# Splitting the first feed-forward's down projection twice for all blocks, with its weights combined in the attention phase and the second feed-forward's on VectorE

## The chip, the core and the metric

One core of a Trainium2 chip runs the kernel. The metric is device time in microseconds (us), the median of several executions. TensorE (PE in the profile) multiplies, VectorE (DVE) and ScalarE (ACT) work element by element, GpSimd (POOL) does too, and SyncE (SP) issues most of the DMAs, in the order in which they stand in its queue.

## The reference

Eight sequences of 512 tokens with 512 channels in float32 go through four residual layers: cross attention with a linear kernel, a feed-forward, a second cross attention, and a feed-forward of merged experts.

```python
def ffn0(x, proj1, b1, proj2, b2):                 # 512 -> 2048 -> 512
    return gelu(x @ proj1.T + b1) @ proj2.T + b2

def ffn1(x, ...):                                  # 8 groups, 192 hidden units each
    w_tg = ...                                     # a token's share for each group, from a router
    gu, dn = gate_up_proj[dominant_experts], down_proj[dominant_experts]
    gate, up = split(einsum("th,goh->tgo", x, gu))
    return einsum("tg,tgi,ghi->th", w_tg, silu(gate) * up, dn)

x = x + tanh(g_xattn[0]) * linear_attention(layernorm(x), ctx)
x = x + tanh(g_ffn[0])   * ffn0(layernorm(x), ...)
x = x + tanh(g_xattn[1]) * cross_attention(layernorm(x), ctx, mask)
x = x + tanh(g_ffn[1])   * ffn1(layernorm(x), ...)
```

## The kernel before

The work is cut into 24 blocks: the attention layer for each of the eight sequences (`xa0`), then the first feed-forward for each (`ff0`), then the second cross attention with the second feed-forward (`ff1`). While one block multiplies, the next one is prepared: its tokens are normalised on VectorE (`normed`, L426), with the reciprocal standard deviation `rstd` from GpSimd (L442), transposed on TensorE (`turn`), and combined into `S` (`token_combinations`).

All large matrix products use Strassen's scheme in its Winograd form: a product of 2 x 2 quarters takes seven smaller products, numbered 1 to 7, in place of eight. It needs sums and differences of the quarters on both sides. On the weight side they are made once and stored in DRAM; on the token side they are made for each block. `combining` (L233) is the weights' four subtractions.

An `ff0` block has four up units (`Ff0Up`), each with seven products of 128 x 256 results (L789), and one down unit. Their hidden activations are the quadrants a11, a12, a21, a22 of `inner`; `combine_inner` (L825) adds s1 and s2 and turns a21 into the difference. The products of a unit run in the order 1, 2, 6, 5, 7, 4, 3, with the last two of a unit put behind the first of the next unit.

There are two forms of the down unit. `Down` (L890) multiplies seven times with 16 matmuls of 128 x 256 results, over 8 chunks (L905). `SplitDown` (L928) applies the scheme a second time to each of the seven products: 49 small products with 4 chunks each, 28 matmuls of 128 x 128 results for each of the seven (L984). For that, `combine` makes four subtractions of the activations for each product (L969 to L972), `at_once` adds the small results together (L998, L1003, L1007), and the weights are read as one continuous stream, 49 tiles of 256 KB a block. The seven products run in the order `SPLIT_ORDER["ff0"]` = 1, 4, 2, 6, 5, 7, 3. Product 2 reads a12, product 6 reads s2. The first two `ff0` blocks (`ONCE = 2`) use `Down`, the other six `SplitDown`; all `ff1` blocks use `SplitDown` with 3 chunks.

Each product's weights come from DRAM into a ring of 16 tiles (`ring`, L132) on SyncE's queue, 16 tiles ahead of TensorE. When a product is issued, the load for the tile that it frees follows.

The combined weights are made by builders, generators that are stepped now and then:

- In the attention phase `tick` steps `build_weights("ff0", ...)` at every third product. It loads raw weights into ring tiles, GpSimd combines them (four operations of 128 x 512), and SyncE stores the seven results: four up units, then four down chunks for the once-split form.
- In the `ff0` phase `build_stream("ff0", ...)` loads the down weights again, in a tile of seven parts (`build_tile`), combines them on GpSimd, combines the result once more (four operations of 128 x 896, L412 to L419), and stores seven slices of 448 KB in the stream. After that the same is done for the second feed-forward: six up units, then three down chunks. It is stepped at every second or third up product.

GpSimd also adds the output bias to each block's tokens (L581), and makes `rstd`. SyncE's queue carries, besides weights and builds, the attention's denominators: `over<-z` writes 1/denominator to DRAM and `spread<-over` reads it back to all partitions (L1132, L1140). A tile scheduler orders the instructions of the engines; an engine named in `in_order` keeps the order of the program, and SyncE always does here. The functions touched, as they are before the change:

Of the kernel before, what the change touches and what calls it, by code (L numbers as in the profile page):

```python
# [21 lines left out]
F32 = mybir.dt.float32  # L22
# [8 lines left out]
P = 128  # L31
# [37 lines left out]
def flamingo_kernel(  # L69
# [60 lines left out]
    RING = 16  # L130

    def ring(name):  # L132
        return work.tile([P, 2, H2], F32, tag="ring", name=name, bufs=RING)

# [125 lines left out]
    raw_g = []  # L260
    for c in range(NC):
        raw_g.append(ring(f"raw_g{c}").rearrange("p n f -> p (n f)"))
        nc.sync.dma_start(out=raw_g[c], in_=wg[ts(c, P), :])
# [6 lines left out]
    def order_gate():  # L270
# [12 lines left out]
    SPLIT_ORDER = {"ff0": (1, 4, 2, 6, 5, 7, 3), "ff1": (2, 4, 1, 6, 5, 7, 3)}  # L283
# [3 lines left out]
    ONCE = 2  # L287
# [7 lines left out]
        (ph, kind, i, q): dram.tile([P, 2, H2], F32, tag=f"{ph}_{kind}{i}_{q}", name=f"{ph}_{kind}{i}_{q}")  # L295
        for ph, kind, n in (("ff0", "up", 4), ("ff0", "down", 4), ("ff1", "up", 6))
# [58 lines left out]
    def build_weights(ph, tile7):  # L355

        todo = {
            "ff0": (("up", raw_p1, 4), ("down", raw_p2, 4)),
            "ff1": (("up", raw_gu, 6),),
        }[ph]  # L360
        todo = [(kind, raw, i) for kind, raw, n in todo for i in range(n)]

        def load(kind, raw, i):
            t = tile7(f"{ph}_{kind}{i}")
            raw(t, i)
            return t

        if ph == "ff1":
            for kind, raw, i in todo:
                t = load(kind, raw, i)  # L370
                yield
                yield from in_twos(combining(nc.gpsimd, t))
                for q in range(7):
                    nc.sync.dma_start(out=store[ph, kind, i, q], in_=t[q])
                yield
            return
        t = load(*todo[0])
        yield
        for n, (kind, raw, i) in enumerate(todo):
            following = load(*todo[n + 1]) if n + 1 < len(todo) else None  # L380
            yield from combining(nc.gpsimd, t)
            for q in range(7):
                nc.sync.dma_start(out=store[ph, kind, i, q], in_=t[q])
            yield
            t = following

    def in_twos(steps):
        for n, _ in enumerate(steps):
            if n % 2:
                yield  # L390

    def build_stream(ph, raw, tile7):

        place = [SPLIT_ORDER[ph].index(m) for m in (1, 5, 2, 3, 6, 7, 4)]
        for i in range(SPLIT_CHUNKS[ph]):
            t = tile7(f"{ph}_down{i}")
            w = [t[:, k] for k in place]
            raw(w, i)
            yield
            yield from in_twos(combining(nc.gpsimd, w))  # L400

            b = t.rearrange("p k n (h q) -> p k n h q", q=P)
            b11, b12, b21, b22 = (b[:, :, n, h] for n in range(2) for h in range(2))

            def keep(m, w):
                nc.sync.dma_start(out=stream[ph][:, :, SPLIT_INNER.index(m), i, :], in_=w)

            sub = ALU.subtract
            for m, w in ((1, b11), (2, b21), (3, b22)):
                keep(m, w)  # L410
            yield
            nc.gpsimd.tensor_tensor(b12, b12, b11, sub)  # L412
            keep(5, b12)
            yield
            nc.gpsimd.tensor_tensor(b22, b22, b12, sub)
            keep(6, b22)
            yield
            nc.gpsimd.tensor_tensor(b21, b21, b22, sub)
# [7 lines left out]
    def normed(ph, b, tag):  # L426
# [4 lines left out]
        if ph == "xa0":  # L431
            in_order.add("vector")
# [1112 lines left out]
```

## Time and profile before

| | |
|---|---|
| median of 3 runs | 2104.07 us (2101.84 to 2106.63) |
| profiled execution | 2106.83 us, span of its instructions 2104.7 us |
| TensorE busy (PE) | 2061.6 us |
| VectorE busy (DVE) | 1451.9 us |
| ScalarE busy (ACT) | 596.6 us |
| GpSimd busy (POOL) | 318.0 us |
| DMA | 485.12 MB, mean 230 GB/s |

The span is the time from the first to the last instruction. The attention phase takes up to about 418 us of it, the eight `ff0` blocks up to about 1188 us, the `ff1` blocks the rest. Matmuls are pipelined, so the durations of single ones overlap; the time of a product is the distance between starts, as the chain of waits has it. In a row of a group the parts are: line, engine and operation, output and inputs, shape, count, then busy us and mean ns of one, then the engine's idle time before it and what ended that. In a row of waits they are: who waited for whom, us in total, times, the longest.

### The profile page before, as it was taken

How to read it: one execution, taken by the hardware profiler on the slowest of the kernel's cores; microseconds unless marked ns; L12 is line 12 of the kernel's file. 1: busy time of each engine (PE TensorE's matmuls, PEld its weight loads, DVE VectorE, ACT ScalarE, POOL GpSimd, SP SyncE). 2: the span in 40 equal slices, each digit the busy share in tenths (PEclk: the TensorE clock that was granted, in tenths of full speed). 3: DMA queues.
4: the chain of work that ended last, by engine and by line, in shares of the span. 5: the costliest groups of instructions: out<-in, count | busy, mean ns of one | idle time of the engine just before them, and what ended most of it. 6: DMA issues, size and time to landing. Idle time of an engine off the chain costs nothing.

```text
span 2104.7 us, 34195 instructions
## 1 busy us (share of the span) xinstructions
PE 2061.6 (98%) x12460; PEld 1816.1 (86%) x12460; DVE 1451.9 (69%) x2727; ACT 596.6 (28%) x1236; POOL 318.0 (15%) x260
## 2 busy tenths in 40 slices
PE   8999999999999999999999999999999999999998
PEld 4778887788889998889898989898989889898988
DVE  3688777652528494868667777777777677876768
ACT  3433333222222324132334232213222222222121
POOL 3122111342413112240301010000000010100000
PEclk9999999999999999999999999999999999999999
DMA  7345633696869898888875858686776858585865
GB/s 227 120 155 155 209 132 93 214 306 220 294 220 330 285 307 288 283 298 281 297 248 190 304 163 276 198 264 214 229 237 189 283 170 293 157 284 161 269 204 169
DMA packets 306501, 485.12 MB, mean 230 GB/s; under 512 B 37024, under 2 KB 107840, under 8 KB 302240
## 3 DMA queue, kind: packets, MB, share of 16 engines
q1 hardware_dynamic: 298896, 456.18, 67.7%
q10 hardware_dynamic: 5856, 23.20, 2.9%
q0 software_dynamic: 1584, 3.57, 0.7%
q8 instruction: 100, 1.64, 0.3%
q14 instruction: 65, 0.53, 0.1%
HBM read 406.22 MB, written 76.61 MB: 229 GB/s over the span
## 4 chain that ended last, share of the span: by engine, by line
PE 74%; issue 10%; DVE 7%; DMA 4%; POOL 3%; SPq 1%; ACT 1%; ACTq 0%; POOLq 0%; DVEq 0%
PE x_ff L789 23%; PE w_ff L789 11%; PE x_ff_down L984 9%; PE w_ff_down L984 7%; PE z_ff L789 6%; PE z_ff_down L984 3%; PE v_ff_down L984 3%; PE x_ff_down L905 2%; SPq L60 1%; PE w_ff_down L905 1%; PE pt_ff L458 1%; PE pt_xa L458 1%; PE pst L609 1%; PE pr L654 1%; PE z_ff_down L905 1%
## 5 line engine op out<-in xcount | busy, mean ns | idle before, releaser
L789 PE MATMUL x_ff<-S_ff,w_ff_up 128*128 128x256 f32 x1280 | 304.5, 381 | 1.7 <-ACT u_ff L801 1.7
L789 PE MATMUL w_ff<-S_ff,w_ff_up 128*128 128x256 f32 x1280 | 303.6, 380 | 1.5 <-DVE a_ff L844 1.5
L789 PE MATMUL x_ff<-xnT_ff,w_ff_up 128*128 128x256 f32 x1280 | 294.1, 380 | 0.9 <-ACT u_ff L801 0.9
L801 ACT COPY u_ff<-x_ff 128x512 f32<-128x512 f32 x240 | 139.5, 582 | 539.2 <-PE x_ff L789 520.3
L789 PEld LDWEIGHTS x_ff<-S_ff,w_ff_up 128*128 128x128 f32 x1280 | 239.9, 190 | 42.6 <-issue 6.5
L789 PEld LDWEIGHTS w_ff<-S_ff,w_ff_up 128*128 128x128 f32 x1280 | 239.0, 190 | 34.2 <-DVE a_ff L844 2.3
L789 PEld LDWEIGHTS x_ff<-xnT_ff,w_ff_up 128*128 128x128 f32 x1280 | 238.4, 190 | 32.9 <-ACT u_ff L801 1.8
L789 PE MATMUL z_ff<-xnT_ff,w_ff_up 128*128 128x256 f32 x640 | 151.6, 379 | 0.0
L984 PE MATMUL x_ff_down<-w_ff_down,split_ff_down 128*128 128x128 f32 x1152 | 136.4, 275 | 2.8 <-DVE split_ff_down L972 1.9
L984 PEld LDWEIGHTS x_ff_down<-w_ff_down,split_ff_down 128*128 128x128 f32 x1152 | 132.2, 192 | 3.6 <-DVE split_ff_down L972 2.2
L789 PEld LDWEIGHTS z_ff<-xnT_ff,w_ff_up 128*128 128x128 f32 x640 | 119.8, 190 | 15.3
L849 ACT ACTIVATE a_ff<-a_ff,b_sb 128x256 f32<-128x256 f32 x128 | 58.1, 501 | 155.1 <-DVE a_ff L844 155.0
L984 PE MATMUL w_ff_down<-w_ff_down,split_ff_down 128*128 128x128 f32 x768 | 90.8, 275 | 1.1 <-DVE split_ff_down L972 1.1
L828 DVE TENSOR_TENSOR s_ff<-a_ff,a_ff 128x512 f32<-128x512 f32 x56 | 45.8, 819 | 65.4 <-ACT a_ff L849 65.4
L984 PEld LDWEIGHTS w_ff_down<-w_ff_down,split_ff_down 128*128 128x128 f32 x768 | 88.2, 192 | 1.3 <-DVE split_ff_down L972 1.3
L998 DVE TENSOR_TENSOR part_ff_down<-part_ff_down 128x128 f32<-128x128 f32 x245 | 72.6, 313 | 23.4 <-ACT part_ff_down L1011 17.5
L844 DVE TENSOR_TENSOR a_ff<-w_ff,u_ff 128x512 f32<-128x512 f32 x64 | 43.8, 684 | 60.1 <-ACT u_ff L801 60.1
L872 DVE SCALAR_TENSOR_TENSOR g_ff<-th_ff,x_ff 128x512 f32<-128x512 f32 x48 | 32.9, 685 | 70.4 <-ACT th_ff L871 70.4
L882 DVE TENSOR_TENSOR up_ff<-w_ff,u_ff 128x512 f32<-128x512 f32 x96 | 65.6, 683 | 17.7 <-ACT u_ff L801 17.7
L581 POOL TENSOR_TENSOR x_ff<-x_ff,b_sb 128x512 f32<-128x512 f32 x28 | 39.3, 1408 | 253.5 <-DVE xn_ff L451 253.5
L451 DVE TENSOR_SCALAR xn_ff<-x_ff,mv_ff,rstd_ff 128x512 f32<-128x512 f32 x64 | 41.2, 661 | 48.2 <-PE pt_ff L458 36.4
L984 PE MATMUL w_ff_down<-w_ff_down,s_ff 128*128 128x128 f32 x576 | 70.2, 275 | 0.0
(274 smaller groups left out, 3665.2 us busy)
## 6 DMA issues: line engine op xcount, KB each, us to landing
w_ff_down<-stream_ff SPq DMA_DIRECT2D x582, 256.0 KB
w_ff_up<-ff_up SPq DMA_DIRECT2D x560, 256.0 KB
stream_ff<-build_ff_down SPq DMA_DIRECT2D x49, 448.0 KB
x_ff<-x_ff SPq DMA_DIRECT2D x16, 1024.0 KB
share<-shares SPq DMA_DIRECT2D x64, 256.0 KB
w_ff_down<-ff_down SPq DMA_DIRECT2D x56, 256.0 KB
ff_up<-build_ff_up SPq DMA_DIRECT2D x42, 256.0 KB
spread<-over SPq DMA_DIRECT2D x32, 256.0 KB
```

Of the source, the lines that this page charges most:

```text
L451: nc.vector.tensor_scalar(xn[t], xb[:, t, :], mv[:, t, 0:1], rstd[:, t : t + 1], ALU.subtract, ALU.mult)
L458: nc.tensor.transpose(pt[:, c, :], xn[t][:, ts(c, P)], ident)
L581: nc.gpsimd.tensor_tensor(xb[:, t, :], xb[:, t, :], b2_sb, ALU.add)
L789: nc.tensor.matmul(p[:, n, :], lhsT=w[:, c, ts(n, P)], rhs=moving, **self.mark(m, 2 * n + c),)
L801: nc.scalar.copy(self.s[m], p)
L828: nc.vector.tensor_tensor(s1, a21, a22, ALU.add)
L844: nc.vector.tensor_tensor(h, p, s, ALU.add)
L849: nc.scalar.activation(h[:, n, :], p[:, n, :], AF.Gelu, bias=b1_sb[:, f : f + 1])
L882: nc.vector.tensor_tensor(u, p, s, ALU.add)
L905: nc.tensor.matmul(p[:, t, :], lhsT=a[:, k, ts(t, P)], rhs=w[k // 2][:, k % 2, :], **self.mark(m, 2 * k + t),)
L984: nc.tensor.matmul(p[bank][:, place, :], lhsT=operand[k][:, c, :], rhs=w[at // 4][:, ts(at % 4, P)], start=bank not in opened, stop=True, ...
L998: return lambda: nc.vector.tensor_tensor(m(k), m(k), m(by), ALU.add)
```

## The change

All eight `ff0` blocks use `SplitDown`, and its third and fourth products change places (6 now runs ahead of 2). `combine_inner` follows part (2, 1), product 4, instead of part (1, 2), product 3. The stream of the first feed-forward is built in the attention phase (`build_first`), alternating with the up units, stepped at two of five products; nothing of the first feed-forward is built in its own phase. The weights of the second feed-forward are built in the `ff0` phase at every up product (`build_second`), by VectorE instead of GpSimd, and those instructions keep the order of the program (`in_place`). After its loads a build waits 11 steps (`LAND`) before it combines. The bias addition goes from GpSimd to VectorE, behind each transpose. For `ff0` blocks after the second, statistics and normalisation keep the order of the program. The ring has 9 tiles in the attention phase and 7 more (`ringb`) after it; one tile `build` serves the raw gate weights, the builds, and the `ff1` sums.

```diff
-    RING = 16
+    RING, MORE = 9, 7
+    asked = {"ring": 0}
     def ring(name):
+        n = asked["ring"] % (RING + MORE) if "ringb" in bank else 0
+        asked["ring"] += 1
+        if n >= RING:
+            return bank["ringb"].tile([P, 2, H2], F32, tag="ringb", name=name, bufs=MORE)
         return work.tile([P, 2, H2], F32, tag="ring", name=name, bufs=RING)
+    def build_tile(name):
+        return work.tile([P, 7, 2, H2], F32, tag="build", name=f"build_{name}", bufs=1)
...
-    SPLIT_ORDER = {"ff0": (1, 4, 2, 6, 5, 7, 3), "ff1": (2, 4, 1, 6, 5, 7, 3)}
+    SPLIT_ORDER = {"ff0": (1, 4, 6, 2, 5, 7, 3), "ff1": (2, 4, 1, 6, 5, 7, 3)}
-    ONCE = 2
...
+    def combining_again(ph, i, t, eng):
+        b = t.rearrange("p k n (h q) -> p k n h q", q=P)
+        b11, b12, b21, b22 = (b[:, :, n, h] for n in range(2) for h in range(2))
+        def keep(m, w):
+            nc.sync.dma_start(out=stream[ph][:, :, SPLIT_INNER.index(m), i, :], in_=w)
+        sub = ALU.subtract
+        for m, w in ((1, b11), (2, b21), (3, b22)):
+            keep(m, w)
+        eng.tensor_tensor(b12, b12, b11, sub)
+        yield
+        keep(5, b12)
+        eng.tensor_tensor(b22, b22, b12, sub)
+        yield
+        keep(6, b22)
+        eng.tensor_tensor(b21, b21, b22, sub)
+        yield
+        keep(4, b21)
+        eng.tensor_tensor(b11, b22, b11, sub)
+        yield
+        keep(7, b11)
...
+    def build_first():
+        def load_up(i):
+            t = [ring(f"raw_up{i}_{q}") for q in range(7)]
+            raw_p1(t, i)
             return t
+        up = load_up(0)
+        yield
+        for i in range(4):
+            for n, _ in enumerate(combining(nc.gpsimd, up)):
+                if n == 2:
+                    t = build_tile(f"ff0_down{i}")
+                    raw_p2(placed("ff0", t), i)
                 yield
+            store_up("ff0", i, up)
+            for _ in range(2):
                 yield
+            for n, _ in enumerate(combining(nc.gpsimd, placed("ff0", t))):
+                if n % 2:
+                    yield
+            if i < 3:
+                up = load_up(i + 1)
+            yield from combining_again("ff0", i, t, nc.gpsimd)
             yield
+        streamed.add("ff0")
+    def in_place(steps):
+        while True:
+            in_order.add("vector")
+            more = next(steps, steps)
+            in_order.discard("vector")
+            if more is steps:
+                return
+            yield
+    LAND, GAP = 11, 6
+    def build_second():
+        for i in range(6):
+            t = build_tile(f"ff1_up{i}")
+            seven = [t[:, q] for q in range(7)]
+            raw_gu(seven, i)
+            for _ in range(LAND):
                 yield
+            yield from in_place(combining(nc.vector, seven))
+            store_up("ff1", i, seven)
+            for _ in range(GAP):
+                yield
+        for i in range(SPLIT_CHUNKS["ff1"]):
+            t = build_tile(f"ff1_down{i}")
+            raw_dn(placed("ff1", t), i)
+            for _ in range(LAND):
+                yield
+            yield from in_place(combining(nc.vector, placed("ff1", t)))
+            yield from in_place(combining_again("ff1", i, t, nc.vector))
+            for _ in range(GAP + 2):
+                yield
+        streamed.add("ff1")
...
+        ordered = ph == "ff0" and b > 1
-        if ph == "xa0":
+        if ph == "xa0" or ordered:
             in_order.add("vector")
...
+        def biased(t):
+            nc.vector.tensor_tensor(xb[:, t, :], xb[:, t, :], b2_sb, ALU.add)
-        for t in range(NT):
-            nc.gpsimd.tensor_tensor(xb[:, t, :], xb[:, t, :], b2_sb, ALU.add)
...
-            if (r, c) == (1, 2):
+            if (r, c) == (2, 1):
                 combine_inner(ts(self.i, 2))
...
-                self.sums = second.tile([P, 4, 7, P], F32, tag="sums", name=f"sums_{self.tag}")
+                self.sums = build_tile(f"sums_{self.tag}").rearrange(...)
...
-        if next(ticks) % 3 == 2:
+        if next(ticks) % 5 in (1, 3):
             next(builder, None)
...
-            return [Ff0Up(ph, b, i) for i in range(4)] + [Down(ph, b, NF // 2) if b < ONCE else SplitDown(ph, b)]
+            return [Ff0Up(ph, b, i) for i in range(4)] + [SplitDown(ph, b)]
...
+    bank["ringb"] = stack(tc.tile_pool(name="ringb", bufs=1, reuse_waits="tile"))
+    for _ in range(MORE):
+        next(loads)
...
-        return 5 if ph == "ff0" else 24
+        return 7 if ph == "ff0" else 24
...
         if u.kind == "up":
-            ticks += 1
-            if "ff0" not in streamed:
-                if ticks % 2 == 0:
-                    next(again, None)
-            elif ticks % 3 == 0:
-                next(builder, None)
+            next(builder, None)
```

## The prediction

> **What bounds the kernel now.** I read the page first, for the busy shares and the granted clock.
>
> ```profile
> PE 2061.6 (98%) x12460; PEld 1816.1 (86%) x12460; DVE 1451.9 (69%) x2727; ACT 596.6 (28%) x1236; POOL 318.0 (15%) x260
> ...
> PEclk9999999999999999999999999999999999999999
> ```
>
> TensorE is the bound: a saving must be a shorter matmul stream or fewer gaps in it. So I cut the span at the ends of the feed-forward blocks. The table of stretches gives length, then busy time of PE, PEld, DVE, ACT and POOL, then clock, DMA share and GB/s.
>
> ```profile
> 60.00:418.00 358.00, 344.79 (x1866) 281.69 (x1865) 270.04 (x419) 123.50 (x232) 70.06 (x59) 1.00 0.48 152
> 418.00:505.00 87.00, 85.83 (x398) 75.26 (x397) 33.16 (x43) 16.74 (x38) 28.66 (x17) 1.00 0.80 260
> 505.00:600.00 95.00, 94.22 (x445) 82.66 (x444) 41.29 (x47) 21.57 (x46) 35.58 (x21) 1.00 0.78 253
> 600.00:696.00 96.00, 94.33 (x633) 87.97 (x633) 65.42 (x121) 28.54 (x60) 25.77 (x17) 1.00 0.90 301
> 696.00:790.00 94.00, 94.00 (x634) 88.02 (x633) 65.13 (x128) 29.31 (x62) 17.81 (x13) 1.00 0.89 299
> 790.00:890.00 100.00, 96.20 (x635) 89.82 (x635) 68.37 (x128) 29.43 (x63) 21.18 (x14) 0.98 0.86 284
> 890.00:988.00 98.00, 94.81 (x631) 87.59 (x631) 73.92 (x128) 28.86 (x62) 28.18 (x16) 1.00 0.89 293
> 988.00:1083.00 95.00, 94.36 (x637) 88.04 (x636) 65.42 (x132) 29.34 (x62) 18.82 (x11) 1.00 0.88 291
> 1083.00:1188.00 105.00, 103.03 (x716) 92.56 (x714) 71.63 (x175) 43.19 (x89) 6.47 (x9) 1.00 0.70 231
> 1188.00:2105.00 917.00, 909.81 (x5687) 813.09 (x5685) 675.26 (x1347) 226.39 (x480) 45.34 (x56) 1.00 0.70 223
> ```
>
> Length less PE busy is TensorE's idle time: 13.2 us in the attention phase (first row), 13.2 us over the eight blocks of the first feed-forward (1.2, 0.8, 1.7, 0.0, 3.8, 3.2, 0.6, 2.0), 7.2 us over the whole second one. Only the first two of these stages are touched. The block at 696 has no idle at all, with VectorE at 65 of 94 us: the split form can run without gaps.
>
> Then the chain of waits where the worst block loses time (start, length, what):
>
> ```profile
> 838.04 1.73 POOL build_ff_down L236
> ...
> 840.93 1.49 DVE xn_ff L451
> 842.41 1.67 DVE split_ff_down L969
> ...
> 845.50 1.67 DVE split_ff_down L970
> ...
> 848.77 2.56 DVE split_ff_down L972
> ...
> 854.39 0.61 DVE a_ff L844
> ...
> 855.04 7.99 PE z_ff_down L984 x56
> ```
>
> While GpSimd combines weights, VectorE's own subtractions take 1.67 to 2.56 us; the page's groups and their forms have 0.68 us for the same 128x512 work without it. VectorE falls behind, a_ff (the last quadrant of hidden activations) is late, and TensorE waits before the product with it, which comes third in the down projection. After the stop that product takes 7.99 us instead of 6.25, under a granted clock of 0.79 and 0.64 in the next two stretches of 3 us: 1.7 us more. So GpSimd's 15% are not free; they are paid through VectorE.
>
> **The change, part by part.** Sums are against the profiled execution, 2106.8 us (span 2104.7 and 2.1 around it). It stands 2.8 us above the median of the runs, 2104.07; differences are carried over to the median unscaled.
>
> *1. Two down projections split twice.* From the chain:
>
> ```profile
> 471.14 6.91 PE w_ff_down L905 x32
> ...
> 763.28 6.25 PE x_ff_down L984 x56
> ```
>
> A product of the once-split form (L905) is 32 passes in 6.91 us, of the twice-split form (L984) 56 passes in 6.25 us. Seven of each: 48.4 and 43.75 us. Two blocks save 2 x 4.63 = 9.3 us of matmul stream, on the path. A rule speaks against it: the Trainium skill, "TensorE: Matmul & The Clock Gate", section "Back-to-back issue gap", has a matmul of 128 columns in a stream of weight loads at 81 ns where its columns alone would take 56, a factor of 1.46. An estimate from that: half of a 256-column pass (216 ns, 6.91/32) is 108, times 1.46 is 157 ns, times 392 passes is 61.7 us a block, 13 us more than now, 27 us slower for two. The trace has 6.25/56 = 112 ns, in this very code and with these tiles. I take the trace: -9.3.
>
> These blocks gain VectorE's work (four split combinations of 0.68 us for each of seven products, and their joining: from 33 to 41 us busy to about 65) and weight tiles, 49 of 256 KB instead of 28. The block at 696 carries both, and no idle: 0.
>
> *2. GpSimd leaves the first feed-forward.* It loses 24 bias additions there (1.41 us each in the page's group), the second combining of four down chunks, and all combining for the second feed-forward. Going to VectorE: 24 bias additions in these blocks, 24 + 12 subtractions of 128x512 at 0.68 us, and 12 of 128x896, which the trace shows on GpSimd only; between VectorE's rows of 512 (0.68) and 2048 elements (2.28) the line gives 1.08. Together 16 + 24.5 + 13 = 54 us over eight blocks, about 7 each, less the lengthening by GpSimd that ends. VectorE stays near 65 to 72 of 94 us. The second feed-forward runs at 675 of 917 with hardly more idle per block. Bounds of this step: all idle and the clock loss go (-14.9), or VectorE's added work keeps it all (0) or, with its order now fixed at these instructions, adds up to 5.
>
> *3. Order inside the down projection.* The product that needs the late quadrant moves from third to fourth place, and the combination of the other three quadrants is made one product (1.73 us) earlier. That gives the late quadrant 6.25 us more. The largest single wait, 2.5 us on a_ff L844, is this one. Normalisation kept in order no longer lets statistics for a later block stand on VectorE waiting for their load (8.3 us before the stall at 454).
>
> For 2 and 3 together: I leave the last block its 2.0 us and the others 0.3 each, 4 in all, of 13.2 + 1.7. That is -10.9; I take -10. The cover is VectorE's spare 20 us per block; without it each late combination costs its own 0.7 to 1.1 us.
>
> *4. The waits this adds.* VectorE combines in program order, so a weight that has not landed would hold everything behind it: the split combinations, then TensorE. In the trace the loads take from 605.7 to 612.7 and, for the chunk with 16 of them, from 827.1 to 838.0 until GpSimd can start. The change leaves 11 product steps of 1.73 us, 19 us. On SyncE's queue the stores of the combined weights now wait for VectorE, with the ring's weight loads behind them; the ring runs 16 tiles ahead, 14 us in the down projection (16 x 43.75/49), against a lag of 2 to 5 us. 0. The ring starts with 9 tiles and gets 7 more after one matmul product and five loads of the build: about 6 us after the first product, needed after nine (15.6 us). 0. Its tiles are as many as before after that.
>
> *5. The attention phase.* GpSimd's work here: 16 + 16 subtractions as before (1.33 us), plus 16 of 128x896. Those rows have 2.22 to 2.37 us: +37 us. The eight bias additions of the first two blocks go to VectorE (5.5 us), and four normalisations and one subtraction there get back about 4: 0. DMA: one set of loads less, 28 stores of 448 KB for 28 of 256, +1 MB over a stage whose DMA share is 0.48: 0. What the 37 us can cost shows in the waits of TensorE between 60 and 418:
>
> ```profile
> PE pt_xa L458 <- DVE xn_xa L451: 5.9, 6, 2.2
> PE x_xa_down L905 <- DVE x_xa L921: 2.9, 4, 1.0
> ```
>
> The normalised block xn_xa comes right after rstd from GpSimd, and GpSimd's combinations, held back behind rstd in its queue, all run just then: xn_xa takes 1.49 us at most against 0.54 alone. GpSimd is busy 52 us from 60 to 360 (70 to 418) with 5.9 us of such waits; 37 us more, in proportion, is +4.2. In the changed instruction order the work directly after each rstd is longer in one block, alike in most, and shorter in the last, since a chunk's second half waits for its own stores. From nothing (-1, were the timing luckier) to +10 (every 896-wide operation holding one critical VectorE operation by 0.6 us). I take +3.
>
> SyncE's queue in this phase: each chunk's 7 stores and 4 loads stand before and behind the denominators (over<-z), and in two blocks a store waiting for GpSimd stands ahead of spread<-over. I estimate a delay of 2 to 3 us; spread is issued 9 to 11 us before VectorE reads it, and about half of that is landing. 0.
>
> *6. The second feed-forward.* Sums now lie in the build's tile, one buffer as before. 0.
>
> Sum: -9.3 - 10 + 3 = -16.3. Profiled execution 2090.5; median 2087.8, so 2088.
>
> **Rivals.**
> *A. The stalls stay.* VectorE's 54 us and the added order take the place of GpSimd's disturbance; 4 stops for another 4. Then -9.3 + 3: 2097.8. For it: idle appears where VectorE has 68 to 74 busy, and the change moves towards that. Against: the gaps stand beside lengthened operations (the chain above), and the second feed-forward is as loaded without them.
>
> *B. The attention phase pays with its chain: slower.* GpSimd works in order, and rstd stands behind combinations that wait for stores, which stand on SyncE's queue behind over<-z. In the trace rstd starts every 41 us (193.6, 234.0, 277.7) and over<-z goes out 10 us after it. For the tightest chunk: stores out at +15, landed near +22, three more operations to +29, next rstd at +41: 12 us of room. Each us beyond it delays xn, the transposes and TensorE one for one. To turn 16.3 gained into over 4.2 lost takes 20.5 us more, 5 in each of four chunks: the chain must be 17 us longer than I count, in all. Then 2108.5 or more.
>
> *C. Better.* Attention costs nothing, all idle of the first feed-forward goes: -9.3 - 13.2 - 1.7 gives 2080.
>
> That the change does not do what it says is excluded by its instruction order: 392 matmuls of 128x128 replace 224 of 128x256, and only rstd is left to GpSimd in the first feed-forward.
>
> **How the numbers follow.** Main case 0.60 (2081 to 2095); A 0.20 (2094 to 2102); B or another new wait 0.12 (2101 to 2115); C 0.08 (2077 to 2081). 0.2% is 4.2 us, about what a measurement of this kernel can tell from no change, so "same" is 2099.9 to 2108.3. Faster: main, C and about 0.14 of A: 0.82. Same: the rest of A and a little of B: 0.08. Slower: 0.10. The range from 2079 to 2101 leaves out most of B and part of C.
>
> **What would show it.** Right: products of 6.25 us in the first two blocks, no GpSimd line but rstd between 418 and 1188, blocks 94 to 95 us apart, split combinations at 0.68 us, no wait for a_ff ahead of the down projection's fourth product, TensorE's idle in the first feed-forward near 4. Attention: its end within 3 us of before, xn_xa still near 1.0 us mean. Wrong: VectorE waiting on build loads, TensorE waiting on VectorE's splits as often as before (A), or rstd or xn_xa waits above 10 us in the attention phase (B).

## The result and the profile after

The changed kernel takes 2096.51 us (median of six runs, 2095.86 to 2096.93); the kernel before 2108.57 (2101.84 to 2111.61), of which three runs are those of the table before (median 2104.07) and the other three took 2110.5 to 2111.6. The ratio is 0.9947, with a 95% interval of 0.9929 to 0.9965: faster by 0.5%, some 12 us between these medians, and by the interval 7 to 15. The profiled execution of the changed kernel took 2096.49 us (span 2094.7), against 2106.8 (span 2104.7) before: 10.0 us between the spans, which is what the two traces have to account for.

First the page's busy shares and clock.

```profile
PE 2053.7 (98%) x12796; PEld 1821.1 (87%) x12796; DVE 1511.3 (72%) x2965; ACT 610.8 (29%) x1264; POOL 171.1 (8%) x164
PEclk9999999999999999999999999999999999999999
```

TensorE still bounds. VectorE has gained 59 us of work, GpSimd has lost 147. Then the table of stretches (columns: length, busy time of PE, PEld, DVE, ACT, POOL, clock, DMA share, GB/s): first the attention phase before, then the changed kernel, cut at the ends of its stages and blocks.

```profile
56.30:402.20 345.90, 332.69 (x1810) 271.02 (x1809) 266.06 (x409) 116.99 (x219) 64.53 (x51) 1.00 0.46 147
```

```profile
56.10:410.90 354.80, 336.27 (x1810) 273.89 (x1809) 281.40 (x417) 117.98 (x220) 93.40 (x65) 0.99 0.51 156
411.00:503.00 92.00, 92.00 (x617) 86.21 (x616) 55.85 (x120) 28.29 (x58) 0.00 (x0) 1.00 0.90 297
503.00:597.00 94.00, 94.00 (x635) 88.02 (x634) 66.83 (x140) 29.32 (x62) 1.03 (x1) 1.00 0.82 269
...
879.00:979.00 100.00, 96.11 (x628) 89.00 (x627) 68.82 (x141) 28.90 (x62) 1.01 (x1) 0.97 0.84 266
979.00:1074.00 95.00, 95.00 (x643) 88.99 (x643) 73.32 (x157) 29.76 (x64) 2.50 (x2) 1.00 0.89 300
1074.00:1178.00 104.00, 102.49 (x712) 91.94 (x711) 73.46 (x178) 42.75 (x90) 6.48 (x9) 1.00 0.74 244
1178.00:2095.00 917.00, 909.65 (x5686) 812.89 (x5684) 675.33 (x1347) 226.45 (x480) 45.39 (x56) 1.00 0.70 223
```

Three things are to be seen. Most blocks of the first feed-forward have no idle at all (length equals PE busy). The one from 879 lost 3.9 us and some clock. And the attention phase, first row of each table, has 18.5 us of idle where it had 13.2: it ends at 411 and no longer at 402 (the 418 given for the kernel before lies already in its first feed-forward block). The same 1810 matmuls also keep TensorE busy for 336.3 us instead of 332.7. That is the clock: both kernels have one short stretch of half clock near 81 us, the changed one two more, each right behind three us in which TensorE was busy for 1.7 and 1.1 us only.

```profile
203.00:207.00 4.00, 4.00 (x16) 3.38 (x15) 4.00 (x6) 2.80 (x6) 2.04 (x2) 0.66 0.00 0
391.00:395.00 4.00, 4.00 (x18) 3.39 (x17) 4.00 (x8) 1.16 (x3) 0.00 (x0) 0.69 0.72 265
```

Stage by stage, from the start of each stage's first `z` product to that of the next (`z_q` for attention, `z_ff` for the feed-forwards; us of the profiled executions):

| stage | before | after | difference |
|---|---|---|---|
| start | 56.3 | 56.1 | -0.2 |
| attention phase | 345.9 | 354.8 | +8.9 |
| first feed-forward | 785.6 | 766.8 | -18.8 |
| second feed-forward, to the end | 916.9 | 917.0 | +0.1 |

So the gain is that of the first feed-forward, and half of it is given back in the attention phase: 5.3 us of the 8.9 as idle, most of the rest as lost clock. TensorE's waits between 60 and 412 in the changed kernel (in total, times, longest), and what the tile's view has of the operation waited for (min/median/max in ns), first before, then after:

```profile
PE pt_xa L500 <- DVE xn_xa L491: 11.8, 8, 2.4
PE x_xa_down L956 <- DVE x_xa L972: 4.0, 3, 1.7
```

```profile
L451 DVE TENSOR_SCALAR xn_xa<-x_xa,mv_xa,rstd_xa x28: 441/996/1492, 76.2 to 326.2; 128x512 f32<-128x512 f32 x28
```

```profile
L491 DVE TENSOR_SCALAR xn_xa<-x_xa,mv_xa,rstd_xa x28: 442/1479/2296, 75.9 to 335.1; 128x512 f32<-128x512 f32 x28
```

The same VectorE instruction on the same tiles has a longest of 2.30 us instead of 1.49, and the waits on it doubled from 5.9 to 11.8. The timeline of one place shows how (start, length, operation, in brackets the idle before it):

```profile
117.01 1.01 POOL L60 TENSOR_TENSOR rstd_xa<-var_xa,neg_half 128x4 f32<-128x4 f32 x1 [34.23 <-DVE var_xa L478]
...
117.99 8.56 POOL L60 TENSOR_TENSOR build_ff_down<-build_ff_down 128x896 f32<-128x896 f32 x4
118.06 4.51 DVE L491 TENSOR_SCALAR xn_xa<-x_xa,mv_xa,rstd_xa 128x512 f32<-128x512 f32 x2
...
122.62 0.66 PE L500 MATMUL pt_xa<-ident,xn_xa 128*128 128x128 f32 x4 [1.56 <-DVE xn_xa L491]
```

GpSimd has four 128x896 subtractions queued behind rstd, 8.56/4 = 2.14 us each, and two xn_xa beside them take 4.51/2 = 2.26 us each instead of the 0.54 that they take without company (run 1): one GpSimd instruction per VectorE instruction, in step. The transposes (L500), and the products behind them, wait.

The loss in the block from 879, in the chain of waits, then VectorE's row from the timeline and the stretches after the stop:

```profile
882.19 8.97 DMA stream_ff<-build_ff_down
...
891.18 0.04 DVE build_ff_down L60
...
892.19 0.70 DVE a_ff L895
...
892.93 3.78 PE w_ff L840 x8
896.71 2.76 PE z_ff L840 x8
```

```profile
891.18 1.09 DVE L60 TENSOR_TENSOR build_ff_down<-build_ff_down 128x896 f32<-128x896 f32 x1 [7.66 <-DMA stream_ff<-build_ff_down]
```

```profile
893.00:896.00 3.00, 3.00 (x7) 2.45 (x8) 3.00 (x5) 1.54 (x4) 0.00 (x0) 0.50 0.85 230
896.00:899.00 3.00, 3.00 (x9) 2.36 (x8) 3.00 (x8) 0.00 (x0) 0.00 (x0) 0.56 1.10 355
```

VectorE's second subtraction of a second-feed-forward chunk (b22, in place) overwrites what the store issued just before is still reading, and its order is fixed: it stands until that store has landed, 7.7 us, with a_ff behind it and TensorE behind a_ff. Two products of 1.73 us then take 3.78 and 2.76: the granted clock was 0.50 and 0.56 in the two stretches of 3 us after the stop.

### The profile page after: what moved, and what is told of

The parts are those of the page before. It is cut to its first block, busy times and chain, and to the rows that moved or that the text cites. A ratio compares the mean times of both kernels' runs of the same rounds, so it can differ in the third digit from the quotient of the medians.

```text
span 2094.7 us, 35097 instructions
## 1 busy us (share of the span) xinstructions
PE 2053.7 (98%) x12796; PEld 1821.1 (87%) x12796; DVE 1511.3 (72%) x2965; ACT 610.8 (29%) x1264; POOL 171.1 (8%) x164
## 4 chain that ended last, share of the span: by engine, by line
PE 90%; DVE 4%; DMA 3%; issue 1%; POOL 1%; ACT 0%; SPq 0%; ACTq 0%; DVEq 0%; POOLq 0%
PE x_ff L840 26%; PE w_ff L840 13%; PE x_ff_down L1035 13%; PE w_ff_down L1035 8%; PE z_ff L840 6%; PE z_ff_down L1035 4%; PE v_ff_down L1035 4%; PE x_xa_down L956 2%; PE x_q L840 2%; PE pt_ff L500 1%; PE x_g L840 1%; PE pt_xa L500 1%; PE w_xa_down L956 1%; PE w_g L840 1%; DMA stream_ff<-build_ff_down 1%
## 5 line engine op out<-in xcount | busy, mean ns | idle before, releaser
L840 PE MATMUL w_ff<-S_ff,w_ff 128*128 128x256 f32 x1280 | 305.4, 381 | 4.2 <-DVE a_ff L895 4.2
L840 PE MATMUL x_ff<-S_ff,w_ff 128*128 128x256 f32 x1280 | 304.3, 380 | 0.0
L840 PE MATMUL x_ff<-xnT_ff,w_ff 128*128 128x256 f32 x1280 | 294.6, 379 | 0.0
L840 PEld LDWEIGHTS x_ff<-S_ff,w_ff 128*128 128x128 f32 x1280 | 240.5, 190 | 40.1 <-issue 5.0
L840 PEld LDWEIGHTS w_ff<-S_ff,w_ff 128*128 128x128 f32 x1280 | 240.0, 191 | 37.4 <-DVE a_ff L895 5.0
L840 PEld LDWEIGHTS x_ff<-xnT_ff,w_ff 128*128 128x128 f32 x1280 | 237.7, 190 | 31.1 <-ACT u_ff L852 0.5
L840 PE MATMUL z_ff<-xnT_ff,w_ff 128*128 128x256 f32 x640 | 152.6, 381 | 0.0
L840 PEld LDWEIGHTS z_ff<-xnT_ff,w_ff 128*128 128x128 f32 x640 | 120.7, 192 | 15.8
L1035 PE MATMUL x_ff_down<-w_ff_down,a_ff 128*128 128x128 f32 x672 | 80.4, 275 | 0.0
L1035 PEld LDWEIGHTS w_ff_down<-w_ff_down,s_ff 128*128 128x128 f32 x672 | 79.4, 192 | 0.8
```

The costliest lines, as they stand in the source:

```text
L840: nc.tensor.matmul(p[:, n, :], lhsT=w[:, c, ts(n, P)], rhs=moving, **self.mark(m, 2 * n + c),)
L1035: nc.tensor.matmul(p[bank][:, place, :], lhsT=operand[k][:, c, :], rhs=w[at // 4][:, ts(at % 4, P)], start=bank not in opened, stop=True, ...
```

## The experiments

In every case the profiled execution's stages are given beside the median, since the attention phase alone varies: in the five kernels below that leave it as the change made it (runs 4, 5, 6, 8, 9) it took 355.2 to 359.1 us in the profile, with three to five times 3.4 us of half clock. Each stage length is that of one execution. The kernel before was measured beside the experiments, with medians of 2106.0 to 2107.3 us; the changed kernel was not, so a difference of 2 or 3 us from its 2096.51 is not to be read.

**1. Does the attention phase lose by GpSimd running beside xn_xa?** The combinations wait for the block's last xn_xa.

```
         nc.gpsimd.tensor_tensor(rstd, var, neg_half, ALU.pow)
+        held_back.append(b)              # attention blocks after the first; the builder rests
...
             turn(t)
+            if t == NT - 1:
+                nc.gpsimd.tensor_tensor(after_xn, xn[t][:, 0:NT], neg_half, ALU.mult)
+                held_back.clear()        # the builder catches up
```

> The attention phase's GpSimd combinations start only once all four xn_xa of the block exist (a 128x4 operation on GpSimd that reads the last one stands ahead of them). Same combinations, same order, same stores; the whole result is computed. T1, GpSimd disturbs VectorE: each xn_xa that starts beside a GpSimd combination lasts until that instruction ends, so without company it takes near 0.54 us instead of 1.23 mean, TensorE's waits on xn_xa fall from 11.8 us to under 3, and the time from about 2096.5 to about 2088 (2086 to 2091). T2, the stores and loads on SyncE's queue are what lengthened this phase: they stay, waits for x_xa and spread remain, time 2096 to 2098. T3, GpSimd runs out of room when its work starts later, and rstd stands behind it: rstd to xn waits of over 3 us in several blocks, 2097 or more.

Measured: 2097.49 us (2095.05 to 2100.34), ratio to before 0.9956 (0.9942 to 0.9971): no gain. The tile's view and TensorE's waits from 60 to 412 of this kernel:

```profile
L496 DVE TENSOR_SCALAR xn_xa<-x_xa,mv_xa,rstd_xa x28: 445/540/547, 76.6 to 333.4; 128x512 f32<-128x512 f32 x28
```

```profile
PE pt_xa L505 <- DVE xn_xa L496: 4.4, 3, 2.5
PE x_q L849 <- ACT u_q L861: 4.1, 3, 2.2
PE pt_ff L505 <- DVE a L1233: 3.9, 1, 3.9
```

The mechanism of T1 holds to the letter: no xn_xa takes more than 0.55 us. Its price does not: attention took 353.4 us, 1.4 less. The combinations have moved beside other work of the phase: in the changed kernel, then in this one,

```profile
L1198 DVE SCALAR_TENSOR_TENSOR th<-th,spread 128x512 f32<-128x512 f32 x32 | 21.8, 744 | 0.0
```

```profile
L1207 DVE SCALAR_TENSOR_TENSOR th<-th,spread 128x512 f32<-128x512 f32 x32 | 26.1, 876 | 0.0
```

and new waits stand where the old ones went. So freeing xn_xa alone does not bring the loss back. Run 12 takes up the new waits.

**2. What do the sixteen wide subtractions cost in all?**

```
     def combining_again(ph, i, t, eng):
+        def op(dst, x, y):
+            if ph == "ff1":
+                eng.tensor_tensor(dst, x, y, ALU.subtract)
```

> Leaves out the sixteen 128x896 subtractions that GpSimd does in the attention phase (the second combination of the first feed-forward's down weights); loads and stores stay as they are. T1, these operations and what stands behind them cost the phase 8.7 us: the phase ends where it did before the change or earlier, time 2087 to 2090. T2, the loss comes from stores and queues: under 2 us less, 2095 to 2097. Between (2090 to 2095) the 128x512 combinations, which moved to other places under the normalisation, carry the rest.

Measured: 2083.29 us (2082.46 to 2085.67), ratio 0.9888 (0.9873 to 0.9902), 13.2 less than the changed kernel. Attention took 341.7 us, 13.1 less; the other stages did not move (766.9 for the first feed-forward).

```profile
PE pt_xa L503 <- DVE xn_xa L494: 5.0, 6, 2.2
```

The waits on xn_xa are about what they were before (5.9). Stores and loads were all kept, so T2 falls, though the stores no longer stand for GpSimd here, and this run does not tell that apart. The wide subtractions, with what stands behind them, cost 13.1 us for 35.3 us of GpSimd's time, 0.8 us for each, more than the whole phase lost: the rest of the change saved some 4 us in it (341.7 against 345.9 before).

**3. Their time or their length?** The same work in shorter instructions.

```
+        def op(dst, x, y):
+            for k in (slice(0, 7),) if ph == "ff1" else (slice(0, 4), slice(4, 7)):
+                eng.tensor_tensor(dst[:, k], x[:, k], y[:, k], ALU.subtract)
...
-        eng.tensor_tensor(b12, b12, b11, sub)
+        op(b12, b12, b11)
...                                   # likewise the other three
```

> Each 128x896 subtraction of the attention phase becomes two, of 128x512 and 128x384. Same work, same stores. T1a, a VectorE operation waits for the one GpSimd instruction in progress: xn_xa beside them falls from 2.2 to about 1.3 us each, time 2 to 4 us less (2092.5 to 2094.5). T1b, what counts is GpSimd's total time, with rstd behind it: one more issue per operation, 0 to +2 us (2096.5 to 2098.5). T2, stores and queues: no change.

Measured: 2090.46 us (2089.51 to 2091.35), ratio 0.9921 (0.9908 to 0.9933), 6.0 less: more than T1a's range. Attention took 347.9 us.

```profile
L494 DVE TENSOR_SCALAR xn_xa<-x_xa,mv_xa,rstd_xa x28: 439/1459/1490, 76.6 to 330.9; 128x512 f32<-128x512 f32 x28
```

The longest xn_xa is 1.49 us, as it is beside 128x512 combinations before. GpSimd works longer in all (32 of 1.39 us and 16 of 1.16, 63 us, for 57.4 us of the same combinations) and the phase is 7 us shorter. Stores and GpSimd's total work are as before or more, so at least this half of the 13.1 us is the length of the single instruction: how long it holds the VectorE instruction that came upon it.

**4. The stop at the store.**

```
-            yield from in_place(combining_again("ff1", i, t, nc.vector))
+            yield from in_place(combining_again("ff1", i, t, nc.vector, 5))
...
         keep(5, b12)
+        for _ in range(pause):
+            yield
         eng.tensor_tensor(b22, b22, b12, sub)
```

> Five product steps of room between the third store of a second-feed-forward chunk and VectorE's first subtraction that overwrites a stored part (b22). T1, VectorE stands for 7.7 us at 883 until those stores have landed, a_ff behind it and TensorE behind that, and half clock follows: the block at 878 falls from 100.9 to about 94 us, time about 2089.5 (2088.5 to 2091). T2, that block is long because VectorE has too much to do in it, or the same wait comes back at the next subtraction: 2095 to 2097.

Measured: 2089.11 us (2087.56 to 2090.30), ratio 0.9912 (0.9898 to 0.9926), 7.4 less. The first feed-forward took 758.7 us, 8.1 less, attention 355.9. The chain where the stop was:

```profile
885.90 5.18 PE x_ff L842 x24
891.08 1.73 PE w_ff L842 x8
892.80 1.73 PE z_ff L842 x8
```

No wait, full clock. T1 holds; the waits on a_ff are gone from this stage. The other two chunks of the second feed-forward show no such stop in either kernel.

**5. The order of the down projection's products.**

```
-    SPLIT_ORDER = {"ff0": (1, 4, 6, 2, 5, 7, 3), ...
+    SPLIT_ORDER = {"ff0": (1, 4, 2, 6, 5, 7, 3), ...
...
-            if (r, c) == (2, 1):
+            if (r, c) == (1, 2):
                 combine_inner(ts(self.i, 2))
```

> The changed kernel with the first feed-forward's old order of products in the down projection (1, 4, 2, 6, 5, 7, 3), and the combination of the three early quadrants one product later, as before; everything else as changed. The whole result is computed. TA, the order is what cured the stops before the late quadrant's product: a wait of 1 to 2.5 us on a_ff in most of the eight blocks, blocks of 95 to 97 us instead of 93.9, time 2103 to 2112. TB, GpSimd's leaving cured them (VectorE no longer falls behind): blocks stay at 93.9, 2095.5 to 2098.

Measured: 2097.27 us (2091.82 to 2100.30), ratio 0.9950 (0.9934 to 0.9966). The blocks are 92.1, four times 93.9, 99.4, 94.3 and 104.0 us apart, as with the new order but for the sixth (100.9). TB: in this kernel the new order brings nothing.

**6. GpSimd's company in the first feed-forward.**

```
-            yield from in_place(combining(nc.vector, seven))
+            yield from in_place(combining(nc.gpsimd, seven))
...                                   # likewise combining and combining_again of the down chunks
```

> The changed kernel with the second feed-forward's weights combined on GpSimd again (same places in the program, 36 operations of 128x512 and 12 of 128x896 over the eight blocks); bias, order and ordered normalisation as changed. The whole result is computed. TA, GpSimd's company is what made VectorE late: VectorE's subtractions beside it at 1.2 to 2.5 us, waits on a_ff and split in several blocks, +5 to +10 against the changed kernel without its 7 us stop at the stores (which goes, since VectorE no longer stands there): 2094 to 2100. TB, the order of products alone is enough, and GpSimd's company costs nothing: blocks of 93.9 throughout, 2088.5 to 2090.5, as with the room between store and subtraction.

Measured: 2096.59 us (2094.42 to 2100.01), ratio 0.9949 (0.9935 to 0.9964). The stop at 882 is gone, and blocks are 92.1, 93.9, 94.5, 95.4, 95.3, 94.7, 98.6 and 103.6 us apart: 768.0 for the stage against run 4's 758.7, both without the stop. TensorE's waits from 412 to 1178:

```profile
PE x_ff L840 <- ACT u_ff L852: 3.1, 4, 1.3
PE w_ff L840 <- DVE a_ff L895: 2.2, 3, 1.0
PE z_ff_down L1035 <- DVE split_ff_down L1023: 1.2, 1, 1.2
```

TA: GpSimd's 48 combinations, 79 us busy in this trace, cost 9.3 us here, and moving this work to VectorE was worth that, less the 8.1 of the stop that came with it.

**7. Room at the store and still shorter GpSimd instructions.**

```
+            for n in range(2):                      # combining: each 128x512 as two of 256, on GpSimd
+                eng.tensor_tensor(dst[:, n], x[:, n], y[:, n], ALU.subtract)
...
+            for k in (slice(0, 7),) if ph == "ff1" else (slice(0, 2), slice(2, 4), slice(4, 6), slice(6, 7)):
+                eng.tensor_tensor(dst[:, k], x[:, k], y[:, k], ALU.subtract)
```

> The room between store and subtraction in the second feed-forward's chunks, and GpSimd's operations of the attention phase cut finer: each 128x512 into two of 128x256, each 128x896 into four of up to 128x256. The whole result is computed. T1a, a VectorE operation waits for the one GpSimd instruction in progress, so its length sets the wait: xn_xa mean from 1.23 to about 0.9 us, waits on it from 11.8 to 4 to 6 us; 2089.1 with the room alone, less the 6.0 that halves gave, less 2 to 4 more: 2079.5 to 2082. T1b, cutting has reached its end with halves, and more issues in GpSimd's queue push rstd: 2083 to 2086.

Measured: 2083.36 us (2078.72 to 2089.46), ratio 0.9895 (0.9879 to 0.9911), 5.7 less than run 4. Attention took 344.0 us in the profiled execution, the fastest of the six runs; the others took 3 to 11 us more.

```profile
L502 DVE TENSOR_SCALAR xn_xa<-x_xa,mv_xa,rstd_xa x28: 441/942/1043, 77.1 to 327.3; 128x512 f32<-128x512 f32 x28
```

xn_xa follows GpSimd's piece again (0.83 us for 256 elements; longest xn_xa 1.04), so T1a has the mechanism, while the time lies in T1b's range: the finer cut gains no clear time over halves (2083.4 against 2090.5 less run 4's 7.4).

**8. The fixed order of normalisation.** In blocks 2 to 7 of the first feed-forward.

```
-        if ph == "xa0" or ordered:
+        if ph == "xa0":
             in_order.add("vector")
...                                   # and around the xn instructions
```

> The changed kernel without the fixed order of normalisation on VectorE in blocks 2 to 7 of the first feed-forward (its instructions are placed by the scheduler again); all else as changed, the whole result is computed. TA, without it statistics stand on VectorE waiting for their block's load, the splits behind them: stops of 1 to 8 us, 2098 to 2106. TB, it carries nothing: 2095.5 to 2098.

Measured: 2095.59 us (2093.78 to 2100.81), ratio 0.9943 (0.9930 to 0.9956), the stage 766.6 us. TB: it carries nothing here.

**9. The bias on GpSimd again**, beside run 4's room.

```
+            eng = nc.gpsimd if b > 1 else nc.vector
-            nc.vector.tensor_tensor(xb[:, t, :], xb[:, t, :], b2_sb, ALU.add)
+            eng.tensor_tensor(xb[:, t, :], xb[:, t, :], b2_sb, ALU.add)
```

> The kernel with room between store and subtraction (2089.1), and the bias additions of the first feed-forward's blocks 2 to 7 on GpSimd again, 24 of 128x512; the whole result is computed. TA, company of GpSimd costs in proportion to its busy time: the second combination's 74 us there cost 9.3 us over these blocks, so 24 of 1.41 us cost about 4: 2092 to 2095, blocks of 94 to 95 us. TB, one bias addition at a time right after its xn meets little of VectorE: 0 to 1.5, 2088.5 to 2090.5.

Measured: 2090.33 us (2088.55 to 2092.93), ratio 0.9926 (0.9912 to 0.9939); the stage took 758.6 us, run 4's 758.7. TB. GpSimd's busy time alone is no price: 24 single additions of 1.32 us, one behind each xn, met nothing that TensorE waits for, where run 6's combinations, several in a row, did.

**10. The wide subtractions on VectorE**, in the attention phase, with room there too.

```
-            yield from combining_again("ff0", i, t, nc.gpsimd)
+            yield from combining_again("ff0", i, t, nc.vector, 3)
```

> The kernel with room (2089.1), and the attention phase's sixteen 128x896 subtractions on VectorE, with three builder steps between store and first overwrite; the whole result is computed. TA, on VectorE each costs its own 1.08 us (17 us in a phase where VectorE is busy 278 of 351) and holds nobody: of the 12.6 us that leaving them out saves, some 7 to 12 come, 2077 to 2082. TB, VectorE, in the order that the scheduler gave it, stands at the wait for a store or for GpSimd's first combination with the attention's work behind it: 2084 or more.

Measured: 2098.50 us (2096.64 to 2101.16), ratio 0.9964 (0.9951 to 0.9978), 9.4 more than run 4. Attention took 364.0 us. Two groups of this kernel by line (busy, mean ns, then idle before and its releasers):

```profile
L382 DVE TENSOR_TENSOR build_ff_down<-build_ff_down 128x896 f32<-128x896 f32 x4 | 4.3, 1084 | 5.1 <-POOL build_ff_down L60 5.1
...
L387 DVE TENSOR_TENSOR build_ff_down<-build_ff_down 128x896 f32<-128x896 f32 x4 | 4.3, 1076 | 6.5 <-DMA stream_ff<-build_ff_down 6.5
```

TB, worse than it said: 17 us more of VectorE, and it stood 11.6 us for GpSimd and for stores. That TensorE's longest wait on xn_xa is 5.7 us here, where it was 2.4, fits that; which of these stops cost how much was not tried apart.

**11. and 12. Loads that stand in ScalarE's queue.** Runs 1 and 7 showed waits for u_q, with ScalarE's queue standing at an x load that waits for a store.

```
-        queue = nc.scalar if ph == "xa0" and b > 1 else nc.sync
+        queue = nc.gpsimd if ph == "xa0" and b > 1 else nc.sync
```

> The kernel with fine GpSimd pieces and room (2083.4), with the loads of the attention phase's x blocks issued from GpSimd's queue instead of ScalarE's; the whole result is computed. TA, ScalarE's queue stands at the load, which waits for the store of the buffer's former block, with u_q behind it (one wait of 2.7 us in the kernel with fine pieces, with its half clock behind it): that wait goes, 2 to 5 us less, 2078 to 2081. TB, GpSimd stands at the load instead and its combinations slide under the next normalisation: 2083 to 2087.

> The kernel whose GpSimd combinations wait for the block's last xn (2097.5), with the x loads issued from GpSimd's queue; the whole result is computed. TA, what took the place of the waits on xn was ScalarE standing at the load behind a slowed store (x_q waiting for u_q, 4.1 us over three places, and what follows): those waits go, 4 to 8 us less, 2089.5 to 2093.5. TB, the phase is as long for another reason: GpSimd's work itself, wherever it stands, costs its collisions: 2095.5 to 2098.5.

Measured: run 11 (with run 7's edits) 2069.01 us (2064.79 to 2070.81), ratio 0.9819 (0.9805 to 0.9832); run 12 (with run 1's) 2085.51 us (2083.57 to 2089.44), ratio 0.9907 (0.9893 to 0.9920). Both beat TA's range, but the profile puts the gain elsewhere. The waits for u_q are gone, but the attention phase took 345.0 us in run 11 (344.0 in run 7) and 353.4 in run 12 (353.4 in run 1). What got shorter is the start, 46.5 and 45.8 us instead of 57.3 and 56.8. That is 11.0 of the 12.0 us between the medians of runs 12 and 1, so TA fails there; for run 11 it is 10.8 of 14.4, and since run 7's profile is its fastest execution, a gain of TA's size in attention is not excluded. ScalarE's waits from 0 to 60, in the changed kernel:

```profile
ACT v L60 <- DMA w_o<-in_wo: 8.4, 1, 8.4
```

This wait (8.6 us in the kernel before) is not there in run 11. With the loads on ScalarE, the first of them goes out at 0.74 us, beside the loads that the start needs, and the second at 30.08 us in run 7, right before v; on GpSimd's queue the first goes out at 57.2. Which of the two, the early load or the stop before v, made the start longer was not tried apart. TensorE's waits from 0 to 60 in run 7, then in run 11:

```profile
PE pk L60 <- ACT ctxT L60: 4.5, 1, 4.5
PE pctx L60 <- DMA ctx<-in_ctx: 3.7, 1, 3.7
```

```profile
PE pk L60 <- DMA w_k<-in_wkv: 1.5, 1, 1.5
```

This is a cost that both kernels had and the change did not touch. For the attention phase, run 12 leaves TB: with GpSimd's work held back, the phase is as long without the waits on ScalarE as with them. Where those 353.4 us go against run 2's 341.7 was not taken apart further. Run 11 is the fastest version tried, 37 us below the kernel before measured beside it (2106.01). Against the changed kernel's profile, its start is 9.6, its attention phase 9.8 and its first feed-forward 8.2 us shorter.

## Why the prediction was right or wrong

It forecast 2088 and a range of 2079 to 2101; the time lies in the range, 8.5 us above the forecast. Between the medians 12.1 us were gained where 16.3 were forecast, between the profiled executions 10.0 of span. The side was right and the chief mechanism too. Three terms of the sum were mis-sized, in part against each other. That the time fell inside the range is luck in part: had steps 2 and 3 brought the 10 us forecast and not 17.6, the time would have been some 2104, outside the range.

*Step 1, two down projections split twice, -9.3.* Right. A product in the first block, from the changed kernel's chain:

```profile
454.21 6.25 PE x_ff_down L1035 x56
```

The rule of 81 ns against 56 (the Trainium skill, "TensorE: Matmul & The Clock Gate", "Back-to-back issue gap") would have made it 8.8 us, 56 times the prediction's 157 ns (81/56 is 1.45, not its 1.46, which changes nothing here); the row of the trace stood. The first two blocks became 6.0 and 5.6 us shorter, 9.3 together by their products, the rest by idle that went.

*Steps 2 and 3, GpSimd leaves, -10.* The sum was too small and its reasons were partly wrong. Without the stop (run 4) the stage is 26.9 us shorter than before; less 9.3, that is 17.6, beyond the step's own bound of 14.9. All idle but 0.4 us went, where I had left 4 us, and idle understated the loss: in the fifth and sixth blocks run 4 is 5.8 and 4.6 us shorter than before where I counted 3.8 and 3.2 of idle, and had found 1.7 of lost clock in the fifth. Of the three edits that I credited together, the order of the products and the ordered normalisation bring nothing in the changed kernel (runs 5 and 8), nor does the bias (run 9). Moving the second feed-forward's combinations brings 9.3 (run 6). The remaining 8.3 is by elimination what none of these runs put back: above all GpSimd's second combining of the first feed-forward's four chunks, with its loads and stores, by itself or together with edits that cost nothing alone. That was not tried, so its cause stays open. The largest single wait, on the late quadrant, which I put down to the third place in the order, was VectorE's lateness beside GpSimd: with the old order and without GpSimd it is not there.

*Step 4, added waits, 0.* This step failed. It named VectorE combining in order and asked whether its loads have landed (they had, with 19 us of room), but looked at the stores only as traffic on SyncE's queue and not as what the next in-place subtraction waits for. Run 4 puts the stop at 8.1 us of the stage, with 7.7 us of VectorE standing and half clock after it. The row for it was in sight: the prediction's own attention part speaks of a chunk whose second half waits for its own stores, and in the kernel before GpSimd stood 53.9 us for just this, at the same second subtraction:

```profile
POOL build_ff_down L415 <- DMA stream_ff<-build_ff_down: 53.9, 5, 40.8
```

*Step 5, the attention phase, +3.* Mis-sized: +8.9 between the profiled executions, within the bounds of -1 to +10 and beside the upper one. The mechanism was the one named. The failing step is the proportion (waits per us of GpSimd's busy time): it takes a wide instruction for more of the same, where each VectorE instruction that comes upon one stands for that instruction's length. The upper bound, 0.6 us for each wide operation, was the nearer working; run 2 has 0.8, of which 0.5 (8.6/16) is idle and the rest busy time of TensorE, with less half clock. The prediction counted no clock in this step. Two of its own signs failed here: attention ended 8.7 us later and not within 3, and xn_xa's mean went to 1.23 us.

A rule of the Trainium skill would have pointed to it. "SBUF — State Buffer", section "SBUF: two separate sides", says that GpSimd and those VectorE instructions that run in a two-port mode or have two inputs in SBUF share a pair of ports, and whichever starts first holds it for its whole instruction. The traces agree where they can: beside pieces of 2.14, 1.39 and 0.83 us the longest xn_xa is 2.30, 1.49 and 1.04. Not every VectorE instruction is held: the statistics ahead of each xn (st_xa, one input) took 0.67 us each on average in both the changed kernel and run 1, four of them in the midst of three wide subtractions. No run shows in which mode xn_xa runs.

*Step 6, the second feed-forward, 0.* Right, +0.1.

So the sum of -16.3 against a measured span of -10.0 is: -9.3 as forecast; -17.6 for -10; +8.1 for 0; +8.9 for +3, and 0 elsewhere. -9.3 - 17.6 + 8.1 + 8.9 is -9.9.

*The rivals.* A, stalls that stay, is out: one new stop, and none of the old. B, the attention phase pays with its chain, came in part. Its sign, waits on xn_xa over 10 us, is there (11.8). At one place the beginning of its very chain: three wide subtractions waited for a store until 192.0 and ran to 198.6, so that var, which VectorE started at 197.85, took 0.78 us instead of 0.11, and rstd started at 198.7. That is under 1 us, in one block, and it stays far from the point from which B decides. By the waits most of the loss is the held xn_xa (5.9 us more of them, and half clock behind); why freeing it alone gave back no more than 1.4 us (run 1) is explained in part only, by the work that is held in its place. C needs both new costs away; run 7, which works on both, has 2083.4 where C said 2080.

## What to carry to other kernels

Price the work that is moved to a second engine by whom its single instructions meet and by their length, not by its busy time: in one stage 24 additions of 1.3 us, one at a time, cost nothing and 48 combinations of 1.3 to 2.4 us, several in a row, cost 9.3; in another sixteen of 2.2 us cost 13. Count the clock behind each new wait too. Where work is updated in place and stored between its steps, an engine with a fixed order must get room between the store and the first overwrite, just as between a load and its first use. And read a gain stage by stage before believing its reason: the runs with the loads moved beat their forecast by shortening a stage that the forecast never spoke of.

## What the runs showed of the hardware beyond that

A GpSimd subtraction cut in two costs GpSimd more but the kernel less: 128x896 took 2.22 us, as 512 and 384 elements 1.39 + 1.16 (run 3, 6.0 us faster); in pieces of 256, at 0.83 us each, a 128x512 one costs 1.66 instead of 1.38, and the further gain was not clear (run 7). A stop of 3.9 us on TensorE cost another 3.1 us by the clock: 0.50 and 0.56 granted over the six us from 893, and full again by 899. In six executions with the same attention phase (355 to 359 us) TensorE's idle was 18.4 to 19.9 us, and the half clock took another 5.1 to 8.5 us of full-speed time (the sum of length times the missing share of the clock).
